# Swapping weights and stream in L0's sums over neighbours, and adding gathered rows on TensorE in L2

## The chip, the cores and the metric

The kernel runs on one core of a Trainium2 chip. The time is the device time of one execution in microseconds (us); the span is what the profile covers from the first instruction to the last. The core's engines each work through their own queue in order: TensorE (PE in the profile; PEld is its loading of weights), VectorE (DVE), ScalarE (ACT), GpSimd (POOL) and SyncE (SP), which here only issues transfers (DMA). A matrix product holds one operand in the array, the weights, and streams the other through it, column by column; its result goes to PSUM. In fp32 each product stands in the profile as two records.

## The reference, cut to what matters

Four layers of a graph network over 3125 nodes with 64 features and 103,125 edges, sorted by destination. Each layer normalizes the running x, applies a relu, runs two passes over the edges, and adds its result to x.

```python
# L0, two passes: a weighted sum over incoming edges, with plain weights W_self, W_neigh
msg = h[src] * edge_weight[:, None]
h_neigh = segment_sum(msg, dst) * inv_deg
h = h @ W_self[l].T + h_neigh @ W_neigh[l].T + b_neigh[l]       # relu after the first
# L1, two passes: m = (h * norm_out)[src] * (a_mu + exp(a_ls) * eps); segment_sum; norm_in, W, b
# L2, two passes, 5 heads of 64 features: attention over incoming edges
xl = (x @ Wl + bl).reshape(n, H, C);  xr = (x @ Wr + br).reshape(n, H, C)
e = leaky_relu(xl[src] + xr[dst], 0.2)
alpha = einsum('ehc,hc->eh', e, att)
a = softmax of alpha over the edges of one destination
out = segment_sum(a[:, :, None] * xl[src], dst).mean(heads) + bias
# L3, two passes: attention with 8 edge types and 4 heads
```

## The kernel before, in words

Edges are cut into tiles of 128 in the order of their destinations. A chunk is a run of tiles whose destinations lie in a window of 128 nodes: 16 tiles in L0 (51 chunks), 18 in L2 (45 chunks), 24 in L1 and L3. The program is written step by step; a scheduler then fixes the order on each engine ahead of the run, apart from instructions that are marked to stay in program order (here DVE's in L0, L1 and L3, by the helper of line 245). On the chip every queue runs in that fixed order.

**L0 gathers nothing.** `dense_pass` runs twice, with l = 0 and 1. For each chunk the first pass builds a dense array `a` of 128 edge slots by 25 blocks of 128 source nodes: `marks` and `factors` make one-hot factors `ol` and `r` on DVE, half a chunk (8 tiles) at a time, in three buffers each; `build` multiplies them (line 603) and ACT copies the result to `a` and the counts to `cnt` (605, 606). `contract` then multiplies `a` by the 25 blocks of the nodes' rows `h_l` (line 612): the 128x128 block of `a` is the weights, 64 features stream. `contracted` copies the sums to `v` (620). `merge` places them in the chunk's window by a product with `sel` (629) and transposes the window's own rows `hw` (633). `carried` passes a sum that crosses a chunk's edge on to the next chunk; `apply` multiplies by the two weight matrices (650, 651) and counts degrees (653); `rows` finishes on DVE and sends `deg` and `hn` to DRAM (545). `red` (line 245) sums `cnt` after each chunk. The first four arrays are kept in SBUF, 47 go to DRAM (`a_d`, 692) and are read again in the second pass (587) into four buffers. Between the passes SP loads `h_l[1]` (736), writes `n_out`, and issues 2 x 34 loads of one column each (`n_out_w`, `n_in`, 740 and 741), after which DVE computes a reciprocal root (743).

**L1** gathers source rows on POOL (line 257), multiplies them by noise `ea` that SP loads, and sums by products (537). Its gather buffers hold 18 groups of four tiles. It needs `n_in` and `n_out_w` only where a chunk's rows are finished.

**L2** treats two tiles at a time (`score`). POOL gathers 400 fp32 values per edge to `g` (nine buffers of six tiles): five heads of 64 scores and two sums each, five more columns, and the node's own features. PE spreads the destination's scores to the edges (`px`, line 983, bf16, 335 columns, PSUM in two buffers). DVE adds `px` to `g` (984), applies relu and the attention vector (986) and sums one head (987); ACT sums the other four heads (991), because `ACT_HEADS = 4`; `top` on DVE (1000) makes `am`. Every nine pairs the chunk is turned (810), scanned on DVE (816, 818, 820 makes `mx`), turned back (822), weighted, and summed on PE by `ao` (254); `heads` and `nodes` finish the nodes' rows, which in the first layer of L2 also get their products for the second (924, 925). **L3** is built in the same way on smaller rows.

Of the kernel before, what the change touches and what calls it, by code (L numbers as in the profile page):

```python
# [8 lines left out]
F32 = mybir.dt.float32  # L9
# [4 lines left out]
OP = mybir.AluOpType  # L14
# [126 lines left out]
def sorted_path(ctx: ExitStack, tc: tile.TileContext, A: dict, out: bass.AP):  # L141
# [54 lines left out]
    a_d = dram.tile([NC0, P, NBK, P], F32, name="a_d")  # L196
# [241 lines left out]
    def spmm_layers():  # L438
        with tc.tile_pool(name="pm", bufs=1) as pm:
# [107 lines left out]
            def dense_pass(lp, l, kept, wT, bias):  # L547
# [8 lines left out]
                with tc.tile_pool(name="dn", bufs=2) as sp, tc.tile_pool(name="dn_ps", bufs=1, space=PSUM) as ps:  # L556
# [25 lines left out]

                    def begin(c):
                        st = dict(c=c, n=tiles0(c), a=kept[c] if c < KEPT_N else sp.tile([P, NBK, P], F32, name="a", bufs=2 if l == 0 else 4))
                        if l:
                            if c >= KEPT_N:
                                nc.sync.dma_start(st["a"], a_d[c])
                        else:
                            if st["n"] < CT0:
                                nc.vector.memset(st["a"], 0.0)  # L590
                            st["oj"], st["wj"] = marks(c)
                            st["f"] = [factors(c, 0, st["wj"])]
                        hw = st["hw"] = sp.tile([P, D], F32, name="hw", bufs=5)
                        nc.sync.dma_start(hw, tabs[l][bass.ds(load_base(c, base0_i), P), :])
                        return st
# [12 lines left out]
                    def contract(st, b):  # L608

                        if b == 0:  # L610
                            st["pv"] = ps.tile([P, D + 1], F32, name="pv", bufs=2)
                        nc.tensor.matmul(st["pv"][:, :D], st["a"][:, b], h_l[l][:, b], start=(b == 0), stop=(b == NBK - 1))  # L612

                    def contracted(st):
                        M = D
                        if l == 0:
                            M = D + 1
                            nc.tensor.matmul(st["pv"][:, D:], st["oj"].rearrange("p t j -> p (t j)"), one, start=True, stop=True)
                        st["v"] = sp.tile([P, D + 1], F32, name="v")
                        nc.scalar.copy(st["v"][:, :M], st["pv"][:, :M])  # L620
                        st["M"] = M
                        sel = st["sel"] = sp.tile([P, P], F32, name="sel")
                        V.tensor_scalar(sel, iota, at0[:, st["c"]:st["c"] + 1], None, op0=OP.is_equal)

                    def merge(st):

                        M = st["M"]
                        acc = ps.tile([P, P], F32, name="acc")
                        nc.tensor.matmul(acc[:M], st["v"][:, :M], st["sel"], start=True, stop=True)
                        st["sums"] = sp.tile([P, P], F32, name="sums", bufs=4)  # L630
                        nc.scalar.copy(st["sums"][:M], acc[:M])
                        pt = ps.tile([D, P], F32, name="pt")
                        nc.tensor.transpose(pt, st["hw"], ident)
                        st["hT"] = sp.tile([D, P], F32, name="hT")
                        nc.scalar.copy(st["hT"], pt)

                    def carried(st):
                        c, M, sums = st["c"], st["M"], st["sums"]
                        if c:
                            picked = sp.tile([P, P], F32, name="picked")  # L640
                            V.scalar_tensor_tensor(picked[:M], iota[:M], step0[:M, c - 1:c], st["before"]["sums"][:M],
# [27 lines left out]
                    KEPT_N = len(kept)  # L669
                    states = {0: begin(0)}  # L670
                    for c in range(NC0 + 4):
                        st, old = states.get(c), states.get(c - 1)
                        if st:
                            st["before"] = old
                        if c + 1 < NC0 and l:
                            states[c + 1] = begin(c + 1)
                        todo = list(range(NBK)) if (old if l == 0 else st) else []
                        of = old if l == 0 else st
                        if l == 0 and st:
                            st["cnt"] = sp.tile([P, CT0, NBK], F32, name="cnt")  # L680
                            pairs = st["n"] // 2
                            for q in range(pairs):
                                if q == 0 and st["n"] > HT:
                                    st["f"].append(factors(c, 1, st["wj"]))
                                if q == min(4, pairs - 1) and c + 1 < NC0:
                                    states[c + 1] = begin(c + 1)
                                build(st, q)
                                for b in todo[:4]:
                                    contract(old, b)
                                todo = todo[4:]  # L690
                            if c >= KEPT_N:
                                nc.sync.dma_start(a_d[c], st["a"])
# [3 lines left out]
                        for b in todo:  # L696
                            contract(of, b)
                        off = 1 if l == 0 else 0
                        late = [states.get(c - off - k) for k in range(4)]
                        if late[3]:  # L700
                            rows(late[3])
                        if late[2]:
                            carried(late[2]), apply(late[2])
                        if late[1]:
                            merge(late[1])
                        if late[0]:
                            contracted(late[0])

            with tc.tile_pool(name="l0", bufs=1) as lp:
                KEPT = 4  # L710
# [1299 lines left out]
```

## Time and profile before

| | |
|---|---|
| median of 10 runs | 8650.73 us (8639.55 to 8659.64) |
| the profiled execution | 8655.86 us, its span 8654.1 us |
| PE, weight loads, DVE, ACT, POOL busy | 54%, 41%, 49%, 28%, 58% of the span |
| L0, first pass | 118 to 866 us from the start of the span |
| L0, second pass | first products at 871.9, last rows at 1588 us |
| L1 | 1588 to 3703 us |
| L2, the pairs of its first and second pass | 3844 to 5110 and 5152 to 6356 us |
| L3, the rest | to 8654 us |
| one gather in L1, mean (line 257) | 974 ns, 0.30 us of issue before each |
| one gather in L3, mean | 984 ns |
| one load of `a` (1.6 MB) in the second pass of L0 | lands about 6.5 us after its issue |

How the profile's lines read: a group names its line, engine and operation, then output and inputs by their names in the program (buffer numbers left out), shapes, and the count; behind the bar stand the busy us, the mean ns of one, the us that the engine stood idle just before them, and what ended that idle time. "Issue" is time in which nothing that the profile shows was waited for. The timeline gives start and length in us. The clock is the share of full speed that TensorE was granted.

### The profile page before, as it was taken

What the parts mean: (1) busy time and instruction counts of PE and PEld (TensorE: products, weight loads), DVE (VectorE), ACT (ScalarE), POOL (GpSimd) and SP (SyncE); (2) the same over time, 40 slices, a digit from 0 to 9 for tenths busy, and PEclk for the clock granted to TensorE, in tenths of its full rate; (3) what the DMA queues carried; (4) which work ended last, traced back from release to release, by engine and by line L of the source; (5) the groups of instructions that cost most, each with busy time, mean ns of one, the idle gap of its engine ahead of it and who ended that gap; (6) DMA issues with size and microseconds to landing.
All of it is one profiled execution on the core that took longest, in us unless ns stands there. A gap on an engine that the chain in (4) does not pass through costs nothing. (4 is left out here: it accounts for less than half of the span.)

```text
span 8654.1 us, 104742 instructions
## 1 busy us (share of the span) xinstructions
PE 4660.8 (54%) x23937; PEld 3564.7 (41%) x23937; DVE 4272.6 (49%) x12144; ACT 2397.4 (28%) x15657; POOL 5044.3 (58%) x4849
## 2 busy tenths in 40 slices
PE   5998799544444444445656555555563444423333
PEld 4997699433333333323333323333342333322222
DVE  5766011222222222269999988888853333333333
ACT  2333000000000000037777767777641111100000
POOL 0000000377777777727777757777727777677776
PEclk8999555555555555555555555555555555555555
DMA  2332333221111111136555545555532222111111
GB/s 64 119 127 104 97 129 135 61 53 53 53 51 51 52 52 52 47 114 172 164 164 161 161 125 162 159 160 159 158 99 44 49 49 49 46 38 40 40 40 39
DMA packets 542968, 799.05 MB, mean 92 GB/s; under 512 B 253426, under 2 KB 386153, under 8 KB 530315
## 3 DMA queue, kind: packets, MB, share of 16 engines
q0 software_dynamic: 206464, 439.52, 20.0%
q1 hardware_dynamic: 335883, 352.72, 12.8%
q8 instruction: 209, 3.42, 0.2%
q14 instruction: 412, 3.38, 0.1%
HBM read 657.39 MB, written 134.39 MB: 91 GB/s over the span
## 5 line engine op out<-in xcount | busy, mean ns | idle before, releaser
L257 POOL DMA_INDIRECT g<-l,idx x1616 | 1574.6, 974 | 2092.0 <-issue 1963.4
L991 ACT ACTIVATE junk<-g 128x66 f32<-128x66 f32 x6448 | 1558.6, 245 | 348.9 <-issue 101.8
L537 PE MATMUL acc<-hit,g 128*128 128x128 f32 x3232 | 838.8, 441 | 1249.8 <-DVE g L245 1249.8
L537 PEld LDWEIGHTS acc<-hit,g 128*128 128x128 f32 x3232 | 719.9, 328 | 1361.8 <-DVE g L245 1309.8
L991 ACT ACTIVATION_READ_ACCUMULATOR junk<-g 128x1 f32 x6448 | 1212.2, 188 | 0.2
L257 POOL DMA_INDIRECT g<-l_0l,src_t x806 | 919.8, 1141 | 464.4 <-issue 197.4
L257 POOL DMA_INDIRECT g<-l_1l,src_t x806 | 961.4, 1193 | 310.1 <-issue 192.9
L257 POOL DMA_INDIRECT g<-l_0v,idx x806 | 793.3, 984 | 388.4 <-issue 216.7
L257 POOL DMA_INDIRECT g<-l_1v,idx x806 | 793.3, 984 | 284.8 <-issue 212.3
L245 DVE TENSOR_TENSOR g<-g,ea 128x256 f32<-128x256 f32 x404 | 179.0, 443 | 1539.0 <-DMA g<-l,idx 1539.0
L984 DVE TENSOR_TENSOR g<-g,px 128x670 f32<-128x670 f32 x806 | 672.3, 843 | 280.2 <-DMA g<-l_1l,src_t 142.3
L612 PEld LDWEIGHTS pv<-h_l,a 128*128 128x128 f32 x4700 | 792.2, 262 | 43.8 <-ACT a L605 28.3
L612 PE MATMUL pv<-h_l,a 128*128 128x64 f32 x4700 | 800.9, 347 | 15.8 <-ACT a L605 13.4
L983 PE MATMUL px<-win,oT 36*128 36x335 bf16 x1612 | 571.8, 459 | 276.6 <-DVE g L984 231.9
L986 DVE SCALAR_TENSOR_TENSOR g<-g,att 128x660 f32<-128x660 f32 x806 | 671.4, 835 | 0.0
L245 DVE TENSOR_TENSOR am<-am,g 128x16 f32<-128x16 f32 x404 | 74.7, 185 | 1001.7 <-DMA g<-l_1v,idx 548.1
L254 PE MATMUL acc<-ao,g 128*70 128x72 f32 x3224 | 442.2, 328 | 207.1 <-DVE ao L1032 103.9
L254 PEld LDWEIGHTS acc<-ao,g 128*70 128x70 f32 x3224 | 399.4, 235 | 334.9 <-DVE ao L1032 206.0
L254 PE MATMUL acc<-oh,g 128*68 128x12 f32 x3224 | 399.0, 268 | 219.7 <-DVE g L245 99.0
L254 PEld LDWEIGHTS acc<-oh,g 128*68 128x68 f32 x3224 | 380.7, 230 | 260.9 <-issue 96.6
L1252 PE MATMUL px<-win,oT 36*128 36x32 bf16 x1612 | 134.4, 191 | 634.0 <-DVE oT L852 589.0
L540 ACT COPY sums<-acc 128x128 f32<-128x128 f32 x68 | 18.1, 266 | 1621.5 <-PE acc L537 1591.2
(327 smaller groups left out, 7319.9 us busy)
## 6 DMA issues: line engine op xcount, KB each, us to landing
a_d<-a SPq DMA_DIRECT2D x47, 1600.0 KB
a<-a_d SPq DMA_DIRECT2D x47, 1600.0 KB
g<-l,idx POOLq DMA_INDIRECT x1616
ea<-in_edge_attr_dram SPq DMA_DIRECT2D x33, 768.0 KB
ea<-in_edge_attr_n_dram SPq DMA_DIRECT2D x33, 768.0 KB
oT<-dl_d SPq DMA_DIRECT2D x88, 162.0 KB
oT<-dl_d SPq DMA_DIRECT2D x66, 216.0 KB
g<-l_0l,src_t POOLq DMA_INDIRECT x806
```

Of the source, the lines that this page charges most:

```text
L245: return tc.keep_in_program_order(op(*args, **kwargs))
L254: nc.tensor.matmul(acc[..., bass.ds(at, width)], lhsT, rhs, start=False, stop=True, skip_group_check=True)
L257: nc.gpsimd.indirect_dma_start(out=to, out_offset=None, in_=table, in_offset=bass.IndirectOffsetOnAxis(ap=idx, axis=0))
L537: nc.tensor.matmul(st["acc"][:M], g[:, k, :], h[:, k, :], start=(i == 0 and k == 0), stop=(end and k == 3))
L540: nc.scalar.copy(st["sums"][:M], st["acc"][:M])
L612: nc.tensor.matmul(st["pv"][:, :D], st["a"][:, b], h_l[l][:, b], start=(b == 0), stop=(b == NBK - 1))
L983: nc.tensor.matmul(px[:, j, :SW], s["oT"][:, q * P:(q + 1) * P], s["win"][:, i, :], start=True, stop=True)
L984: nc.vector.tensor_add(g[:, :, :SW], g[:, :, :SW], px[:, :, :SW])
L986: nc.vector.scalar_tensor_tensor(g[:, :, :F], g[:, :, :F], 0.0, bcast(att08[l], 1, 2), op0=OP.max, op1=OP.mult)
L991: nc.scalar.activation(junk, g[:, j, hd * C2:(hd + 1) * C2], AF.Copy, accum_out=al[:, q0 + j, hd:hd + 1])
L1252: nc.tensor.matmul(px[:, k * H * R:(k + 1) * H * R], s["oT"][:, q * P:(q + 1) * P], s["win"][:, q // 2, :], start=True, stop=True)
```

## The change

In L0, arrays now stand for two chunks, 256 slots wide. `contract` holds the nodes' rows (64 columns) as weights and streams 256 slots, so that the sums come out transposed, 64 by 256, and the new step `turned` turns each half back by a product with the identity. Steps after it follow a table of due times. `a` has two buffers of double size, the loads of `n_in` and `n_out_w` and their roots move from between L0's passes to the start of L1, and `hw` is loaded later. In L2, PE adds the gathered row to `px` by a product with the identity, in fp32, ahead of line 983's; ACT copies the five score columns back to `g`; line 986 reads `px` in PSUM; and `ACT_HEADS` is 3, so that DVE sums two heads and ACT three.

In the order on PE the 25 products of a pair of chunks come in one block after the pair's 32 products of `build` in the first pass of L0; before, 25 of every second chunk came in a block and the others between those of `build`.

```diff
-    a_d = dram.tile([NC0, P, NBK, P], F32, name="a_d")
+    a_d = dram.tile([(NC0 + 1) // 2, P, NBK, 2 * P], F32, name="a_d")
...
                     def begin(c):
-                        st = dict(c=c, n=tiles0(c), a=kept[c] if c < KEPT_N else sp.tile([P, NBK, P], F32, name="a", bufs=2 if l == 0 else 4))
-                        if l:
-                            if c >= KEPT_N:
-                                nc.sync.dma_start(st["a"], a_d[c])
...
+                        p, i = divmod(c, 2)
+                        if i == 0:
+                            arrays[p] = kept[p] if p < len(kept) else sp.tile([P, NBK, 2 * P], F32, name="a", bufs=2)
+                            if l and p >= len(kept):
+                                nc.sync.dma_start(arrays[p], a_d[p])
+                        st = dict(c=c, n=tiles0(c), a=arrays[p][:, :, i * P:(i + 1) * P])
...
-                        hw = st["hw"] = sp.tile([P, D], F32, name="hw", bufs=5)
-                        nc.sync.dma_start(hw, tabs[l][bass.ds(load_base(c, base0_i), P), :])
...
-                    def contract(st, b):
+                    def contract(p, b):
 
                         if b == 0:
-                            st["pv"] = ps.tile([P, D + 1], F32, name="pv", bufs=2)
-                        nc.tensor.matmul(st["pv"][:, :D], st["a"][:, b], h_l[l][:, b], start=(b == 0), stop=(b == NBK - 1))
-
-                    def contracted(st):
-                        M = D
+                            sums_of[p] = ps.tile([D, 2 * P], F32, name="pv", bufs=2)
+                        nc.tensor.matmul(sums_of[p], h_l[l][:, b], arrays[p][:, b], start=(b == 0), stop=(b == NBK - 1))
+
+                    def contracted(p):
+                        v = sp.tile([D, 2 * P], F32, name="vT")
+                        nc.scalar.copy(v, sums_of[p])
+                        sums_of[p] = v
+
+                    def turned(st):
+                        c = st["c"]
+                        M = st["M"] = D if l else D + 1
+                        pt = ps.tile([P, D + 1], F32, name="pn")
+                        nc.tensor.transpose(pt[:, :D], sums_of[c // 2][:, c % 2 * P:(c % 2 + 1) * P], ident[:D, :D])
                         if l == 0:
-                            M = D + 1
-                            nc.tensor.matmul(st["pv"][:, D:], st["oj"].rearrange("p t j -> p (t j)"), one, start=True, stop=True)
-                        st["v"] = sp.tile([P, D + 1], F32, name="v")
-                        nc.scalar.copy(st["v"][:, :M], st["pv"][:, :M])
...
+                            nc.tensor.matmul(pt[:, D:], st["oj"].rearrange("p t j -> p (t j)"), one, start=True, stop=True)
+                        st["v"] = sp.tile([P, D + 1], F32, name="v", bufs=3)
+                        nc.scalar.copy(st["v"][:, :M], pt[:, :M])
+                        sel = st["sel"] = sp.tile([P, P], F32, name="sel", bufs=3)
+                        V.tensor_scalar(sel, iota, at0[:, c:c + 1], None, op0=OP.is_equal)
+                        hw = st["hw"] = sp.tile([P, D], F32, name="hw", bufs=4)
+                        nc.sync.dma_start(hw, tabs[l][bass.ds(load_base(c, base0_i), P), :])
...
-                        acc = ps.tile([P, P], F32, name="acc")
+                        acc = ps.tile([P, 2, P], F32, name="acc")
...
-                        pt = ps.tile([D, P], F32, name="pt")
-                        nc.tensor.transpose(pt, st["hw"], ident)
+                        nc.tensor.transpose(acc[:D, 1], st["hw"], ident)
...
-                    for c in range(NC0 + 4):
+                    lag = 1 - l
+                    np_ = (NC0 + 1) // 2
+                    due = {}
+                    for n in range(2 * (np_ + lag) + 6):
...
+                            todo = [(p, b) for b in (range(NBK // 2) if i == 0 else range(NBK // 2, NBK))]
...
-                                for b in todo[:4]:
-                                    contract(old, b)
-                                todo = todo[4:]
+                                for t in todo[:2]:
+                                    contract(*t)
+                                todo = todo[2:]
...
+                        if 0 <= p < np_ and i == 1:
+                            contracted(p)
+                            both = [states[c] for c in (2 * p, 2 * p + 1) if c < NC0]
+                            for j, s_ in enumerate(both):
+                                for k, f in ((1, turned), (2 + j, merge), (3 + j, carried), (3 + j, apply), (4 + j, rows)):
+                                    due.setdefault((n + k, f), []).append(s_)
...
-                KEPT = 4
-                kept = [lp.tile([P, NBK, P], F32, name=f"kept{c}") for c in range(KEPT)]
+                KEPT = 2
+                kept = [lp.tile([P, NBK, 2 * P], F32, name=f"kept{c}") for c in range(KEPT)]
...
                     if l == 0:
...
                         nc.sync.dma_start(h_l[1], by_block(tabs[1]))
-                        n_out_d, deg_d = tables["n_out"], tables["deg"]
...
-                        for c in range(NCH):
-                            nc.sync.dma_start(n_out_w[:, c:c + 1], n_out_d[bass.ds(load_base(c), P), :])
-                            nc.sync.dma_start(n_in[:, c:c + 1], deg_d[bass.ds(load_base(c), P), :])
-                        with tc.tile_pool(name="nrm", bufs=1) as np_:
-                            nc.vector.tensor_copy(n_in, rsqrt(np_, n_in, [P, NCH]))
...
                     nc.sync.dma_start(by_block(tabs1[0]), h)
+                for c in range(NCH):
+                    nc.sync.dma_start(n_in[:, c:c + 1], deg_d[bass.ds(load_base(c), P), :])
+                    nc.sync.dma_start(n_out_w[:, c:c + 1], n_out_d[bass.ds(load_base(c), P), :])
+                with tc.tile_pool(name="nrm2", bufs=1) as np_:
+                    nc.vector.tensor_copy(n_in, rsqrt(np_, n_in, [P, NCH]))
...
-        ACT_HEADS = 4
+        ACT_HEADS = 3
...
                     for j in range(2):
                         q = q0 + j
-                        nc.tensor.matmul(px[:, j, :SW], s["oT"][:, q * P:(q + 1) * P], s["win"][:, i, :], start=True, stop=True)
-                    nc.vector.tensor_add(g[:, :, :SW], g[:, :, :SW], px[:, :, :SW])
+                        nc.tensor.matmul(px[:, j, :SW], ident, g[:, j, :SW], start=True, stop=False)
+                        nc.tensor.matmul(px[:, j, :SW], s["oT"][:, q * P:(q + 1) * P], s["win"][:, i, :], start=False, stop=True)
+                    nc.scalar.copy(g[:, :, F:SW], px[:, :, F:SW])
                     HV = H - ACT_HEADS
-                    nc.vector.scalar_tensor_tensor(g[:, :, :F], g[:, :, :F], 0.0, bcast(att08[l], 1, 2), op0=OP.max, op1=OP.mult)
+                    nc.vector.scalar_tensor_tensor(g[:, :, :F], px[:, :, :F], 0.0, bcast(att08[l], 1, 2), op0=OP.max, op1=OP.mult)
```

## The prediction

> **What bounds the kernel now.** I read the slices of the span first, to see which engine is full where; then the busy times by stretch, one stretch per pass; then PE's timeline for its pitch, and the costliest groups for L2.
>
> ```profile
> POOL 0000000377777777727777757777727777677776
> PEclk8999555555555555555555555555555555555555
> ```
>
> Tenths of each fortieth of the span. GpSimd (POOL), which issues the gathers, works from L1 on; TensorE's (PE) granted clock is full in the first L0 pass alone.
>
> ```profile
> 126.00:823.00 697.00, 679.59 (x4605) 634.96 (x4603) 481.12 (x911) 261.31 (x939) 0.00 (x0) 1.00 0.29 114
> ...
> 893.50:943.60 50.10, 0.03 (x1) 0.00 (x0) 1.33 (x7) 0.23 (x1) 0.00 (x0) 0.50 0.08 1
> ...
> 946.00:1588.00 642.00, 641.44 (x2801) 596.60 (x2800) 69.23 (x300) 36.58 (x150) 0.00 (x0) 0.50 0.36 126
> ...
> 3844.00:5110.00 1266.00, 757.74 (x3388) 419.96 (x3386) 1150.55 (x3154) 903.98 (x6720) 911.39 (x799) 0.52 0.58 161
> 5152.00:6356.00 1204.00, 700.32 (x3302) 401.75 (x3302) 1041.38 (x2815) 852.74 (x6585) 956.56 (x801) 0.51 0.58 160
> ...
> 4261.84:4265.26 3.42, 3.42 (x26) 2.90 (x25) 3.42 (x9) 2.10 (x17) 2.54 (x3) 0.50 0.59 169
> 4265.26:4268.68 3.42, 2.75 (x24) 1.69 (x22) 3.09 (x9) 1.92 (x11) 3.12 (x2) 1.00 0.46 112
> ```
>
> Columns: stretch, its length, then busy us of PE, weight loads, DVE, ACT, POOL, then clock, DMA share, GB/s. The second L0 pass is busy 641.44 of 642 us and still gets half a clock: busy is not what opens it. Between the passes PE stands 50 us. Between 3844 and 6356 us, L2, VectorE (DVE) leads: 403 pairs of tiles a layer, 1266/403 = 3.14 us and 1204/403 = 2.99 us each, DVE busy 91% and 86%. The last two lines are one of L2's short stays at full clock: one packed stretch at 0.50, then one at 1.00.
>
> ```profile
> 401.24 3.22 PE L603 MATMUL pa<-r,ol 128*128 128x225 f32 x16
> ...
> 418.85 5.79 PE L612 MATMUL pv<-h_l,a 128*128 128x64 f32 x50
> ...
> 1559.90 10.93 PE L612 MATMUL pv<-h_l,a 128*128 128x64 f32 x50
> ```
>
> An fp32 product is two records. At full clock 225 columns take (3.22-0.35)/15 = 0.19 us a record, 0.85 ns a column; 64 columns should take 0.055 us but take 5.79/50 = 0.116, and 0.219 at half clock, because each record first waits for 128 columns of weights. So the second L0 pass streams about half the time only.
>
> ```profile
> L257 POOL DMA_INDIRECT g<-l_1l,src_t x806 | 961.4, 1193 | 310.1 <-issue 192.9 <-DVE rt L802 64.8 <-ACT junk L991 11.6
> L257 POOL DMA_INDIRECT g<-l_0l,src_t x806 | 919.8, 1141 | 464.4 <-issue 197.4 <-DMA l_0r<-rt 136.8 <-DVE ao L1029 42.8
> ...
> L984 DVE TENSOR_TENSOR g<-g,px 128x670 f32<-128x670 f32 x806 | 672.3, 843 | 280.2 <-DMA g<-l_1l,src_t 142.3 <-PE px L983 110.6 <-DMA g<-l_0l,src_t 10.3
> L986 DVE SCALAR_TENSOR_TENSOR g<-g,att 128x660 f32<-128x660 f32 x806 | 671.4, 835 | 0.0
> L983 PE MATMUL px<-win,oT 36*128 36x335 bf16 x1612 | 571.8, 459 | 276.6 <-DVE g L984 231.9 <-DMA win<-l_0r 14.5 <-DMA win<-l_1r 14.1
> ```
>
> In L2 a pair needs two gathers. POOL issues one every 1.27 us in L1 (0.97 + 0.30 of issue), but they grow to 1.14 and 1.19 us here: 2.9 and 3.0 us a pair. POOL stands right behind DVE in the first layer and sets the pace with it in the second.
>
> **The change, part by part.** The sum is made against the profiled execution, 8655.9 us, 5 above the median of the runs.
>
> *L0, second pass.* Weights become 64 columns, the stream 256: 256 x 0.85 = 0.217 us a record at full clock, 0.435 at half, weights hidden behind it. A pair of chunks is 25 x 2 x 0.217 = 10.9 us, or 21.7 at half. The rest of PE's work is 13.06 (pitch of a chunk now) - 10.93 = 2.1 us at half clock, 2.1 a pair at full; two more turns of the 64 x 256 sums and the waits for their copies, by the 64x128 turn and the 0.22 us copy, about 1.1. Pair: 14.1 us, 26 pairs 367. The stream is then near 80% busy, like the packed stretch that opened the clock in L2, so I take full clock. The array's load for two chunks lands 6.5 us after issue for 1.6 MB now, so at most 12 us for 3.2 MB: under 14, hidden. The pass (871.9 to 1588, 716 us) becomes 372 with its ends: **-344**. This holds the 50 us stall: the 68 one-column loads of n_in and n_out_w (0.82 us apiece on SP's queue) move to L1's start, ahead of the first edge-noise load; 18 buffers of four gathers, 90 us of POOL, cover those 56. Without that cover, +56. Bounds: -380 if the turns hide; -60 if the clock stays half (26 x 25.8 + 50 less stall).
>
> [...]
>
> *L0, first pass.* Its clock is full already. Products: 2 x 5.79 becomes 10.9 a pair, -0.7. But the program's order puts all 25 products in a block behind the pair's 32 one-hot products (L603), where today most stand between those. New waits per pair: the last array copy on ACT before the block (0.49 + 0.21, about 0.8); after it copy, turn, copy, turn (1.7 with the turns' own 0.3). In the odd chunk the factors of its second half come late: DVE first reduces the even chunk's counts (0.96 + 0.19), makes rows (0.9) and carries (0.75), two sel (0.5), then ol and r (1.21 + 0.36 + 1.82), in all 6.7 us after the even chunk's copies; PE has 3.2 us of the first half plus 2.5 of small products to do. About 2 us stand. Sum: 27.5 us a pair now, 31.2 after. In that wait PE streams about a third of the time, and L2's lines show a full clock lost on a thin stretch; half speed for one 3.4 us stretch in six pairs of ten adds 1. +4.7 x 26 = **+122**. Bounds: -20 (all covered by DVE running three halves ahead), +225 (a cold stretch each pair and late hw loads, which SP issues behind deg and hn). Eight instead of five row writes are left at the end, 6.3 us each, partly under the last block: **+12**, 0 to +20.
>
> *L2.* Per pair DVE loses L984 (0.77 start to start); L986 reads PSUM instead, as L984 did at the same rate; L987 takes two heads, 132 more elements, +0.14. DVE falls from 2.86 and 2.58 to about 2.25 and 1.95 us. ACT loses two of its eight sums (0.24 each) and gains one copy of 10 columns, by L620's 65 columns at most 0.22: 2.2 becomes 2.0. PE gains two identity products of 335 columns, four records of 0.285 us = 1.14 at full clock, 2.28 at half, two of L983 (at most 571.8/1612 = 0.35 each now, at half) and about 0.45 or 0.9 of sums and heads: 1.95 or at most 3.9 us a pair. At half clock PE would be full, streaming over 85%, which is what the packed stretch shows opening the clock; at 1.95 of 2.8 us it streams some two thirds, like the first L0 pass (64% there by the same count), which kept it. So PE stays below POOL, and POOL bounds: 2 x (0.97 + 0.30) = 2.55 if gathers run as in L1 (DVE 25% busy), 2.9 and 3.0 as now (DVE 90%). DVE would be about 75% busy; between these I take 2.80, which leaves room for waits on mx and ao. **-(0.34 + 0.19) x 403 = -214.** Bounds: 2.55, -415; PE at half clock, 3.9, +673.
>
> [...] The trace only shows that gathers are longer beside a busy DVE.
>
> L1's gathers and L3 are untouched. Sum: 8656 - 344 + 122 + 12 - 214 = 8232; I say **8235 us**.
>
> **The rivals.**
> 1. *L2's clock does not hold* (the other sign). PE at half speed or flickering becomes L2's bound. For it: L2 has 0.52 and 0.51 today, and PE waits in order on DVE's scans, which thins stretches. Against it: the load that opens it. At 3.9 us a pair: 8656 - 210 + 673 = 9119. It decides from 3.33 us a pair on, where L2 gives back L0's 210.
> 2. *Gathers stay long.* POOL keeps 2.9 and 3.0 us: L2 gives about -90; 8355. For it: the second layer already runs at POOL's pace. Against it: less DVE beside them.
> 3. *L0's second pass stays at half clock.* Then -60 in place of -344: 8516. For it: 640 us at 0.50 now; against it: those stream half the time.
>
> **How the numbers follow.** Chances: forecast 0.58, long gathers 0.18, L0 at half clock 0.08, L2's clock 0.13 (of which 0.03 between 3.1 and 3.33 us a pair), others 0.03. The forecast's own range is 8060 to 8420: L0's first pass gives +-100, L2 -140 to +80. The 80% range adds rivals 2 and 3: 8050 to 8530. Faster than before: 0.58 + 0.18 + 0.08 + 0.02 = 0.86; slower 0.11; within 0.2% (17 us, about what a measurement of this kernel can tell) 0.03.
>
> **What would show it.** Clock 1.0 through the second L0 pass, 14 us a pair, and no 50 us gap; 31 us a pair with a hole before each odd chunk's second half in the first; in L2 a clock mostly 1.0, 2.8 us a pair, gathers near 1.05 us and POOL's idle mostly its issue time. Wrong if L2's clock shows 0.5 with PE full, or if L1's first sums come so late that POOL stops.

## The result: 8907 us, 3.0% slower

The changed kernel takes 8907.48 us (median of 8 runs, 8895.67 to 8925.73) against 8651.34 for the kernel before on the same chips (28 runs): a ratio of 1.030, 95% interval 1.0289 to 1.0307. The forecast was 8235 with a range to 8530. The profiled execution has a span of 8917.6 us, 263.5 more than before. By stages, in us of the span:

| stage | before | after | difference | the prediction's term |
|---|---|---|---|---|
| L0, first pass (to the first load of `a` in the second) | 118 to 872 | 117 to 1319 | +447 | +122 and +12 |
| L0, second pass | 872 to 1588 | 1319 to 1695 | -340 | -344 |
| to L1's first product | 1588 to 1628 | 1695 to 1803 | +68 | 0, or +56 without cover |
| L1, first to last product | 2073 | 2072 | -1 | 0 |
| to L2's first pair | 143 | 136 | -7 | 0 |
| L2, both passes with the gap between | 2510 | 2612 | +102 | -214 |
| the rest | 2300 | 2294 | -6 | 0 |

One term of four was right. The slices of the changed kernel, tenths of each fortieth of the span as before:

```profile
PE   4777769534444444449999998999984444433333
...
POOL 0000000077777777726555555666635777767776
PEclk8877779755555555557888887999985555555555
```

PE's clock is no longer full in the first pass of L0 (7 and 8 where it had 8 and 9), it is full in the second, and in L2 it is mostly granted, but there PE is now 9 tenths busy and POOL only 5 or 6. By stretch (PE, weight loads, DVE, ACT and POOL busy, then clock, DMA share, GB/s), the two passes of L0 and the two of L2:

```profile
117.00:1318.60 1201.60, 896.59 (x3524) 671.87 (x3524) 493.80 (x956) 282.41 (x986) 0.00 (x0) 0.79 0.18 69
1318.60:1695.00 376.40, 366.66 (x1708) 220.63 (x1708) 69.11 (x299) 45.14 (x179) 0.00 (x0) 0.99 0.57 219
4011.00:5389.00 1378.00, 1272.95 (x4999) 602.13 (x4999) 934.36 (x2768) 770.92 (x5528) 792.87 (x804) 0.82 0.54 149
5427.00:6623.00 1196.00, 1103.10 (x4911) 535.83 (x4911) 823.38 (x2418) 711.07 (x5387) 780.43 (x803) 0.92 0.58 161
```

The second pass of L0 does what was forecast: clock 0.99, a pair of chunks every 14.4 us (14.1 forecast). The first pass has PE idle a quarter of the time at a clock of 0.79. L2's loss is all in its first pass: 1378 us for 403 pairs of tiles, 3.42 us each (3.14 before); the second takes 1196, 2.97 each (1202 before). PE is busy 92% in both.

**L0's first pass.** A pair of chunks takes 44 to 49 us in the steady part (47.7 in the one shown below), not 31.2. The waits of 200 to 1200 us (waiting engine, tile and line, what ended it; us in all, times, longest):

```profile
DVE oj L245 <- PE pn L629: 502.6, 22, 24.9
...
PE acc L644 <- DMA hw<-l: 107.8, 20, 7.0
...
PE pa L605 <- DVE r L245: 68.0, 22, 3.1
```

DVE, which works in program order, stands 23 us of each pair before it may write `oj`, and what ends that is L629, the product in the new step `turned` that reads an older `oj`. The same in the timeline:

```profile
460.78 0.35 SPq L635 DMA_DIRECT2D hw<-l  x1
...
467.96 0.40 PE L644 MATMUL acc<-ident,hw 128*64 128x128 f32 x1 [5.49 <-DMA hw<-l]
...
476.30 11.01 PE L616 MATMUL pv<-a,h_l 128*64 128x256 f32 x50 [0.58 <-ACT a L607]
...
488.38 0.29 DVE L245 TENSOR_TENSOR oj<-iota,dl 128x128 f32<-128x128 f32 x1 [24.08 <-PE pn L629]
...
492.32 1.87 PE L605 MATMUL pa<-r,ol 128*128 128x225 f32 x4 [3.09 <-DVE r L245]
```

The block of 25 products ends, is turned, and only then does DVE begin the marks of the next two chunks, so PE stands 3.1 us for its first factors. Earlier in the pair it stands 5.5 us for `hw`, whose load SP now issues in `turned`, one step ahead of its use. With each of these two waits the clock falls to half for 10.2 us, at 464.9 and at 492.2 us (between 200 and 1200 us it falls 43 times, 34 of them for 10.2 us): L605's records, 0.190 us apart on the median at full clock, are 0.374 apart there.

**L1's start.** POOL's first gather comes right behind the last step of `n_in`'s root:

```profile
1792.73 0.18 DVE L767 COPY n_in<-rsq_r 128x34 f32<-128x34 f32 x1
1792.98 0.98 SPq L492 DMA_DIRECT2D ea<-in_edge_attr_dram  x2
1793.96 1.10 POOL L257 DMA_INDIRECT g<-l,idx  x1 [1764.22 <-issue]
```

That root waits for the 68 small loads, which leave SP's queue from 1732 to 1790. So the eighteen gather buffers cover nothing: they are not filled before.

**L2.** The costliest groups:

```profile
L998 PE MATMUL px<-g,ident 128*128 128x335 f32 x3224 | 1488.1, 547 | 77.9 <-DVE g L1002 58.3
L257 POOL DMA_INDIRECT g<-l_0l,src_t x806 | 796.3, 988 | 681.3 <-DVE al L1003 294.3
L257 POOL DMA_INDIRECT g<-l_1l,src_t x806 | 784.2, 973 | 457.8 <-issue 189.2
...
L1002 DVE SCALAR_TENSOR_TENSOR g<-px,att 128x660 f32<-128x660 f32 x806 | 676.5, 839 | 366.2 <-ACT g L1000 351.1
```

Gathers did shorten, from 1141 and 1193 to 988 and 973 ns, yet POOL now waits for others. DVE waits 351 us for ACT's copy of the five score columns (L1000). Read alone, this line says that the copy, queued behind ACT's sums, is the new bottleneck. But the copy in turn waits mostly for PE's last product (331 us between 4100 and 5200 us), and PE waits for almost nothing: it is PE's pace that both lines show. Three records of a tile at full clock:

```profile
4601.24 0.83 PE L998 MATMUL px<-g,ident 128*128 128x335 f32 x2
4602.00 0.31 PE L999 MATMUL px<-win,oT 36*128 36x335 bf16 x1
4602.24 0.83 PE L998 MATMUL px<-g,ident 128*128 128x335 f32 x2
```

A tile takes 1.00 us, 2.0 a pair. The next record starts 0.386 and 0.378 us behind the two fp32 ones, where 335 columns at the 0.85 ns of L603 in L0 come to 0.285: each time that fp32 and bf16 products alternate, some 0.1 us is added. It reads as a wait for the weights: the trace has the loading of such weights start within 0.01 us of their own product, but that of a second fp32 record, at 4601.34, 0.28 us before its own. And once a chunk the clock falls. Columns as in the stretches above:

```profile
4608.62:4612.04 3.42, 2.79 (x9) 1.17 (x9) 3.42 (x10) 1.96 (x16) 2.81 (x3) 1.00 0.68 189
4612.04:4615.46 3.42, 2.04 (x8) 0.76 (x6) 3.42 (x15) 2.95 (x25) 2.51 (x4) 1.00 0.63 183
4615.46:4618.88 3.42, 3.10 (x7) 1.57 (x6) 2.80 (x12) 2.59 (x17) 0.65 (x1) 0.50 0.42 120
4618.88:4622.29 3.41, 3.41 (x12) 1.41 (x11) 0.90 (x2) 0.43 (x2) 0.00 (x0) 0.50 0.14 40
4622.29:4625.71 3.42, 3.42 (x14) 1.83 (x12) 2.72 (x9) 1.91 (x13) 1.83 (x2) 0.50 0.15 30
4625.71:4629.12 3.41, 3.41 (x22) 1.73 (x21) 1.87 (x5) 1.72 (x13) 2.50 (x4) 1.00 0.53 151
```

In the second of these PE stands 1.38 us for one small transposition, and the next three stretches run at half clock:

```profile
4615.24 0.29 PE L932 MATMUL ptn<-ident,tr 85*65 85x85 f32 x1 [1.38 <-DVE tr L925]
```

Over the whole first pass (4011 to 5389 us) this wait comes 43 times:

```profile
PE ptn L932 <- DVE tr L925: 56.8, 43, 1.4
```

The clock falls 43 times there too, 42 times right behind a stretch of 3.41 us whose longest wait is this one, and 40 of the falls last 10.2 us.

So the theory for the experiments was: two buffers of `oj` (and, smaller, the late `hw`) in L0's first pass; the memory of a root at L1's start; and in L2 PE as the bound, by gaps between its products and by the clock. The rivals: `hw` alone in L0, the edge noise's loads in L1, and ACT's copy in L2.

### The profile page after: what moved, and what is told of

Same layout as the page of the kernel before. It is cut to its first block, busy times and chain, and to the rows that moved or that the text cites. A ratio compares the mean times of both kernels' runs of the same rounds, so it can differ in the third digit from the quotient of the medians.

```text
span 8917.6 us, 103400 instructions
## 1 busy us (share of the span) xinstructions
PE 5475.2 (61%) x24763; PEld 3498.7 (39%) x24763; DVE 3837.6 (43%) x11338; ACT 2144.6 (24%) x13293; POOL 4741.1 (53%) x4849
## 3 DMA queue, kind: packets, MB, share of 16 engines
q14 instruction: 386, 3.16, 0.1%
## 5 line engine op out<-in xcount | busy, mean ns | idle before, releaser
L998 PE MATMUL px<-g,ident 128*128 128x335 f32 x3224 | 1488.1, 547 | 77.9 <-DVE g L1002 58.3
L1007 ACT ACTIVATE junk<-g 128x66 f32<-128x66 f32 x4836 | 1173.6, 246 | 178.7 <-DVE g L1002 171.2
L257 POOL DMA_INDIRECT g<-l_1l,src_t x806 | 784.2, 973 | 457.8 <-issue 189.2
L1007 ACT ACTIVATION_READ_ACCUMULATOR junk<-g 128x1 f32 x4836 | 907.9, 188 | 0.0
L1002 DVE SCALAR_TENSOR_TENSOR g<-px,att 128x660 f32<-128x660 f32 x806 | 676.5, 839 | 366.2 <-ACT g L1000 351.1
L998 PEld LDWEIGHTS px<-g,ident 128*128 128x128 f32 x3224 | 546.6, 211 | 322.6 <-issue 225.5
L616 PE MATMUL pv<-a,h_l 128*64 128x256 f32 x2400 | 544.9, 382 | 13.3 <-ACT a L607 13.3
L605 PE MATMUL pa<-r,ol 128*128 128x225 f32 x1612 | 476.1, 461 | 83.7 <-DVE r L245 83.3
L999 PEld LDWEIGHTS <-oT 36*128 36x128 bf16 x1612 | 151.2, 94 | 813.1 <-issue 808.8
L605 PEld LDWEIGHTS pa<-r,ol 128*128 128x128 f32 x1612 | 397.7, 256 | 115.4 <-DVE r L245 78.8
```

The source lines that it names most:

```text
L257: nc.gpsimd.indirect_dma_start(out=to, out_offset=None, in_=table, in_offset=bass.IndirectOffsetOnAxis(ap=idx, axis=0))
L605: nc.tensor.matmul(pa[:, j], ol[:, k + j], r[:, k + j], start=True, stop=True)
L616: nc.tensor.matmul(sums_of[p], h_l[l][:, b], arrays[p][:, b], start=(b == 0), stop=(b == NBK - 1))
L998: nc.tensor.matmul(px[:, j, :SW], ident, g[:, j, :SW], start=True, stop=False)
L999: nc.tensor.matmul(px[:, j, :SW], s["oT"][:, q * P:(q + 1) * P], s["win"][:, i, :], start=False, stop=True)
L1002: nc.vector.scalar_tensor_tensor(g[:, :, :F], px[:, :, :F], 0.0, bcast(att08[l], 1, 2), op0=OP.max, op1=OP.mult)
```

## The experiments

The single runs below stand beside runs of the kernel before of 8655.06 us (the first four) and 8651.74 us (the next four).

**One part alone.** L0 and L1 as before, L2 as changed (the L2 lines of the diff):

> L0 and L1 as before, L2 as changed. The trace of the changed kernel has L2's pairs from 4011 to 6625 us, 2614 us, against 2512 before, with TensorE busy over 90% of them. Theory: L2 loses by itself, +102: 8651 + 102 = about 8755 us. Rival: L2's loss comes with the changed L0 (where buffers lie, the state of the clock on entering); then within 20 us of 8651, or below it.

8728.72 us, +74 on the same chip, less than the +102 expected: L2 takes 1377 and 1175 us in its two passes, in the changed kernel 1378 and 1196. Why the second differs by 21 us is open. L2 loses by itself, all of it in the first pass; the rest of the loss is L0's and L1's start.

**L0's first pass.** Six buffers of `oj`, then the load of `hw` moved back to the chunk's begin, then both:

```diff
-                        oj = sp.tile([P, CT0, W0], F32, name="oj")
+                        oj = sp.tile([P, CT0, W0], F32, name="oj", bufs=6)
```

> The changed kernel with six buffers of oj in place of two. Theory: turned reads oj after the block of 25 products, so with two buffers DVE can't mark the next two chunks until the block is done (DVE stands 23 to 24 us a pair), and the block can't be spread between build's products. With six it is spread, a pair of chunks falls from 47.7 us to 31 to 36, the first pass of L0 from 1132 to 830 to 930, the whole from 8907 to about 8600 to 8710. Rival: a pair is long because merge waits 5.5 us for hw and the clock halves after that; then the pair stays above 42 us and the whole above 8760.

```diff
                             st["f"] = [factors(c, 0, st["wj"])]
+                        hw = st["hw"] = sp.tile([P, D], F32, name="hw", bufs=10)
+                        nc.sync.dma_start(hw, tabs[l][bass.ds(load_base(c, base0_i), P), :])
...
-                        hw = st["hw"] = sp.tile([P, D], F32, name="hw", bufs=4)
-                        nc.sync.dma_start(hw, tabs[l][bass.ds(load_base(c, base0_i), P), :])
```

> The changed kernel with hw loaded where a chunk begins, as before the change, in place of where its sums are turned. Theory of the block: hw's wait is a second, smaller cause; the 5.5 us of it go and half of the half-clock stretch behind it, 6 to 9 us of a pair's 47.7, 25 times: 8680 to 8760. Rival (the wait only moves, since DVE's factors end late anyway): under 30 us gained, 8880 or more.

> Both edits. If hw's load is late by itself, both together give 10 to 100 us more than the buffers of oj alone. If the spread block already gives the load time to land, the same as oj alone within 25 us, the first pass of L0 at 28 to 33 us a pair, close to the 27.5 of before.

The buffers alone: 8590.52 us, 317 less than the changed kernel and already faster than before. `hw` alone: 8810.02, 97 less; a pair falls from some 47 to 41.0 us, as expected, but the first pairs (34 to 36 us in both) gain nothing and the second pass is 10 us longer, so that the whole gained less than the range said. Both: 8586.25, the same as the buffers alone. With six buffers, the scheduler spreads the 25 products between those of `build`; a pair takes 32.0 us, and the pass, between 200 and 850 us, reads:

```profile
200.00:850.00 650.00, 650.00 (x2798) 399.48 (x2796) 395.48 (x755) 220.73 (x789) 0.00 (x0) 1.00 0.27 108
```

PE is busy all of the time at full clock, and no wait for `oj`, `hw` or `r` is left. So the two buffers were the cause; the late `hw` was a second one that only the block brought out. The 32.0 us that stand against 28.2 before (in the steady part as well) are PE's own work: in its mixed order L616's records come 0.260 us apart on the mean against 0.226 in the second pass, and L605's 0.236 against 0.219 before.

**L1's start.** On top of the six buffers, the root's two small tiles go to L1's own pool, which stays, and not to one that is closed before the gather buffers are laid out:

```diff
-                with tc.tile_pool(name="nrm2", bufs=1) as np_:
-                    nc.vector.tensor_copy(n_in, rsqrt(np_, n_in, [P, NCH]))
+                nc.vector.tensor_copy(n_in, rsqrt(lp, n_in, [P, NCH]))
```

> As the run with six buffers of oj (8590.5 us), and the root of n_in in memory that stays, not in a pool closed before L1's gather buffers are laid there. Theory: POOL's first gather (at 1793.96 in the changed kernel, 1.2 us after DVE's last step of the root) waits for that memory; it would start some 56 us earlier, right after the write of h, and since POOL's gathers set L1's pace L1 ends about 56 earlier: 8525 to 8545 us. Rival: the edge noise, whose loads stand on SP behind the 68 small ones, is the limit, and the gathers that are ahead give nothing: 8580 to 8600, with L1's first product and its last where they were.

8534.36 us, 56 less. POOL's first gather, at 1461.21 with six buffers of `oj`, now comes at 1403.25:

```profile
1403.25 1.10 POOL L257 DMA_INDIRECT g<-l,idx  x1 [1372.68 <-DMA n_in<-deg]
```

L1's first product moves by 7 us only, since the edge noise is still loaded behind the 68 small loads. But the gathers run ahead meanwhile, and its last product comes 57 us earlier. What stood was the gathers' memory, and POOL sets L1's pace.

**L2.** All on top of six buffers of `oj` (8590.52 us): the steps from `turn` on one pair later; with that, a pair's products in the order identity, identity, bf16, bf16; or, instead of that order, every third pair added on DVE as before the change.

```diff
-                        (11, heads), (13, nodes)] + [(14 + i, f) for i, f in enumerate(end)])
+                        (11, heads), (13, nodes)] + [(15 + i, f) for i, f in enumerate(end)])
```

> As the run with six buffers of oj (8590.5 us), and in L2 the steps from turn on one pair of tiles later, so that PE does not stand 1.4 us for tr (L932). Theory: that wait leaves one thin 3.4 us stretch a chunk, after which the clock is halved for 10.2 us of 30.7; without it the clock stays, the first pass of L2 falls from 30.7 us a chunk to 24 to 27, 45 chunks: -170 to -300, 8290 to 8420. Rival 1: the clock falls anyway (other waits on the scans): less than 60 us gained. Rival 2: ACT's copy of the score columns behind its sums, which DVE waits for, sets the pace and not PE: less than 60 us gained, with the clock at 1.0.

```diff
                     for j in range(2):
                         q = q0 + j
                         nc.tensor.matmul(px[:, j, :SW], ident, g[:, j, :SW], start=True, stop=False)
+                    for j in range(2):
+                        q = q0 + j
                         nc.tensor.matmul(px[:, j, :SW], s["oT"][:, q * P:(q + 1) * P], s["win"][:, i, :], start=False, stop=True)
```

> As l2turn, and in L2 the two products by the identity first, then the two bf16 ones, of each pair. If PE sets the pace of L2 (its two fp32 records of 335 columns start 0.386 and 0.378 us apart at full clock, 0.1 more than their columns take, since weights aren't loaded ahead between fp32 and bf16), two of four such gaps go, 0.2 us a pair: up to -160 over both passes of L2. If PE doesn't set the pace any more, less than 40 from l2turn.

```diff
-                        nc.tensor.matmul(px[:, j, :SW], ident, g[:, j, :SW], start=True, stop=False)
-                        nc.tensor.matmul(px[:, j, :SW], s["oT"][:, q * P:(q + 1) * P], s["win"][:, i, :], start=False, stop=True)
-                    nc.scalar.copy(g[:, :, F:SW], px[:, :, F:SW])
+                        if i % 3 != 1:
+                            nc.tensor.matmul(px[:, j, :SW], ident, g[:, j, :SW], start=True, stop=False)
+                        nc.tensor.matmul(px[:, j, :SW], s["oT"][:, q * P:(q + 1) * P], s["win"][:, i, :], start=i % 3 == 1, stop=True)
+                    if i % 3 == 1:
+                        nc.vector.tensor_add(g[:, :, :SW], g[:, :, :SW], px[:, :, :SW])
+                    else:
+                        nc.scalar.copy(g[:, :, F:SW], px[:, :, F:SW])
-                    HV = H - ACT_HEADS
-                    nc.vector.scalar_tensor_tensor(g[:, :, :F], px[:, :, :F], 0.0, bcast(att08[l], 1, 2), op0=OP.max, op1=OP.mult)
+                    HV = H - ACT_HEADS - (i % 3 == 1)
+                    nc.vector.scalar_tensor_tensor(g[:, :, :F], (g if i % 3 == 1 else px)[:, :, :F], 0.0, bcast(att08[l], 1, 2), op0=OP.max, op1=OP.mult)
```

In these pairs ACT sums four heads and DVE one, as before the change; the expectation's "three" is a slip.

> As l2turn, but every third pair of tiles adds on DVE as before the change (ACT then with three sums, DVE with one). If PE sets the pace at full clock: PE loses 1.5 us in three pairs of 8.3, DVE gains 0.7 in 7: 60 to 150 us faster than l2turn, POOL (1.25 us a gather, 22.5 a chunk) next. If the thinner stream loses the clock, slower than l2turn by 100 or more.

The two passes of L2, the later step first:

```profile
3676.00:4916.00 1240.00, 1157.56 (x4994) 554.93 (x4995) 936.83 (x2756) 756.60 (x5510) 789.44 (x803) 0.91 0.60 166
4950.00:6183.00 1233.00, 1135.38 (x4913) 549.84 (x4914) 829.40 (x2420) 711.06 (x5389) 779.59 (x803) 0.90 0.58 156
```

then with the products in groups:

```profile
3677.00:4796.00 1119.00, 989.22 (x4996) 526.26 (x4995) 926.70 (x2755) 747.20 (x5513) 791.97 (x804) 0.97 0.66 184
4830.00:5946.00 1116.00, 953.79 (x4911) 513.24 (x4912) 820.82 (x2417) 704.24 (x5386) 783.61 (x803) 0.96 0.64 173
```

and with a third of the pairs on DVE:

```profile
3669.00:5044.00 1375.00, 1305.86 (x4458) 618.11 (x4459) 1002.41 (x2897) 800.47 (x5922) 822.69 (x804) 0.61 0.54 150
5082.00:6453.00 1371.00, 1191.57 (x4377) 565.56 (x4377) 908.59 (x2557) 757.88 (x5796) 786.28 (x802) 0.66 0.52 141
```

and of this run one stay at half clock:

```profile
3737.94:3761.83 23.89, 23.01 (x66) 10.80 (x64) 18.46 (x56) 13.51 (x102) 18.40 (x19) 0.50 0.65 172
```

- *Later step*: 8487.95 us, 103 less, a smaller gain than the 170 to 300 expected. The first pass falls from 1382 to 1240 us with its clock from 0.82 to 0.91. But the theory is only half right: the clock does not stay, it still falls 40 times (43 before), now behind waits of `ao`'s products and of L939, and what has changed is that it is halved for 3.4 us each time, 219 us in all, where it was 498. The second pass, 1192 with the buffers alone, is 1233 here.
- *Groups*: 8250.79 us, 237 less again, which is more than the 160 expected; each pass gains about 120. In the trace a pair's six records now start 0.386, 0.282, 0.282, 0.377, 0.153 and 0.233 us apart, 1.71 in all against 2.01: of the gaps between fp32 and bf16 half are left, and the bf16 pair overlaps too. 403 pairs by 0.30 would be 121 us a pass at full clock. That this meets the gain so closely is partly chance: the clock rose as well, PE is busy 168 and 182 us less in the two passes, and at 88% and 85% busy it no longer sets the pace all of the time. But the edit moves PE's products alone, and neither ACT's copy nor DVE's work, so the rival that these set the pace falls.
- *A third on DVE*: 8752.74 us, 265 more than the later step alone, though PE has 536 records less in either pass. Its clock is 0.61 and 0.66, and PE is busy 95% of the first pass. Once a chunk the clock falls and is back only 24 us later (of 30.7), though PE is busy all but 0.9 of these 24 us, and at half clock a record takes about twice the time (0.374 us in place of 0.190 for L605 in the changed kernel). That it is the thinner stream that loses the clock was expected, but is argued: the run also changes the order of work and its waits.

**The sum.** The four edits together; the same without the later step; and the sum with L0's first pass done as before the change (a's 128x128 blocks as weights, chunk by chunk) into arrays of two chunks for the changed second pass:

> The four edits together. Where the kernel before takes its usual 8650 us, and the gains of the single runs add: 8250.8 - 56 = 8195, 8175 to 8215 us. If L2's gain came by chance of one look: 8380 to 8440. On a chip where the kernel before takes 9900 or more: 10400 to 10500 again, which would say nothing on the sum.

> As best1, but L2's steps from turn on where the change had them. If the wait for tr still thins a 3.4 us stretch and halves the clock a third of the time: 60 to 150 us slower than best1, all in the first pass of L2, clock there 0.80 to 0.90. If the order of the products alone gives PE enough room: within 25 us of best1.

> As best1, but the first pass of L0 sums as before the change. It was 108 us faster than best1 twice where L2 stalled, 85 of them in L0's first pass (708 us of build against 793). If that is all L0: 85 to 110 us faster than best1 here too, 8085 to 8115.

The sum: 8196.61 us (8188.62 to 8201.78), ratio 0.946 to the kernel before (0.9448 to 0.9479), within 2 us of the sum of the single gains. With L0's first pass as before: 8099.17 (8092.72 to 8101.78), ratio 0.935 (0.9337 to 0.9368). That pass takes 709 us of build instead of 792, and the second is unchanged (first and second pass):

```profile
200.00:800.00 600.00, 585.53 (x3944) 545.12 (x3942) 420.46 (x806) 226.79 (x814) 0.00 (x0) 1.00 0.31 121
888.00:1256.00 368.00, 361.52 (x1682) 217.30 (x1682) 65.23 (x282) 43.06 (x171) 0.00 (x0) 0.99 0.58 222
```

So of the change in L0, the wider stream pays only in the second pass, where nothing but the sums is done.

Without the later step: 8238.97 us, 42 more than the sum, between the two cases that had been set. The two passes of L2, without and then with the later step:

```profile
3615.00:4820.00 1205.00, 1066.36 (x4998) 562.72 (x4998) 923.68 (x2769) 754.47 (x5528) 788.59 (x803) 0.89 0.62 171
4857.00:5933.00 1076.00, 922.97 (x4914) 501.33 (x4914) 814.90 (x2419) 703.45 (x5388) 800.96 (x802) 0.99 0.66 179
```

```profile
3620.00:4740.00 1120.00, 992.41 (x4994) 527.45 (x4994) 925.92 (x2756) 746.52 (x5511) 789.52 (x804) 0.97 0.67 184
4774.00:5901.00 1127.00, 965.84 (x4912) 522.06 (x4912) 823.66 (x2419) 704.96 (x5388) 783.13 (x803) 0.95 0.63 171
```

With the later step the first pass gains 85 us and the clock 0.08, so the wait for `tr` does lower the clock there; most of L2's repair is the order of the products. The second pass loses 51 us, with the clock at 0.95 in place of 0.99 (it falls 24 times in place of 6). PE's order there is the same but for its last chunk, but DVE's and ACT's are not, since the later step moves the second pass's last steps as well: in 42 of 44 chunks DVE makes `yo` before the first of a chunk's three products for `ao`, where it made it after the second. Whether that lowers the clock was not tried.

**On two other chips** the same three kernels ran as well, and there the kernel before itself takes 10024.92 and 9890.06 us:

> The changed kernel with the four edits that gained: six buffers of oj, n_in's root in memory that stays, L2's steps from turn on one pair later, and L2's products in the order identity, identity, bf16, bf16. If the gains add (L1's 56 us are in another stage than the others): 8250.8 - 56 = 8195, 8175 to 8215 us. If L1's gain is taken back at L2's start: 8240 or more.

> As best1, but the first pass of L0 sums as before the change (a's 128x128 blocks as weights, 64 features as stream, chunk by chunk), into arrays of two chunks that the second pass then reads as changed. If the turns and the wider order of the first pass cost what the runs show (793 us of build against 705 before, TensorE full at clock 1.0 in both): 60 to 100 us faster than best1, 8095 to 8135. If the writes of two chunks at once, or the smaller lag, stall it: no faster than best1.

> The four edits together, on a chip where the kernel before takes its usual 8650 us (on the chip of the run before this it took 10025, with gathers that landed late through all of L2). If the gains of the single runs add: 8250.8 - 56 = 8195, 8175 to 8215 us, 0.945 to 0.950 of before. If L2's gain came by chance of one look: 8380 to 8440.

On the first of them the sum took 10491.55 us (ratio 1.046, 1.0425 to 1.0489) and the version with the old first pass 10382.78 (1.036, 1.0326 to 1.0389); on the second 10465.63 (1.058, 1.0547 to 1.0617) and 10357.02 (1.047, 1.0437 to 1.0498). The version without the later step took 10457.43 and 10504.82 in single runs. So there both are slower than the kernel before. L0's passes are as long as elsewhere, and the old first pass is worth 109 us (97 elsewhere). Most of the lost time is in L2, 1965 and 1932 us for its passes in place of 1120 and 1127, but not all: of the 2243 us by which the sum's profile is longer on the second of these chips, some 1650 are L2's, 270 L1's with its start, and 330 come behind L2. The waits on both chips have a releaser that no profile from the other chips shows; in the first pass of L2 on the second chip:

```profile
ACT sums L1064 <- remote: 351.3, 36, 13.0
...
DVE ao L1046 <- remote: 243.4, 30, 11.0
ACT g L1001 <- remote: 239.3, 35, 11.3
```

"Remote" is something outside of what the profile follows; each of these three steps is held 30 to 36 times in 45 chunks, for 7 to 10 us on the mean, with the durations of the instructions unchanged (L1003 takes 0.84 us here too). Such waits stand in L1 and L3 as well. Late gathers, which an expectation above names, are not it: between 4000 and 5800 us on the first of these chips DVE waits 15 us for gathers to land. What the releaser is, and why the kernel before loses less (some 1370 and 1240 us against its usual time, the sum 2290 and 2270), was not found, and the changed kernel was not run beside them.

## Why the prediction was wrong, point by point

- *L0's second pass, -344*: right, -340, and by its reason. The stream of 256 columns runs at clock 0.99 (0.216 us a record, 0.217 forecast), the weight loads are busy 220.63 of 376.40 us, where they were 596.60 of 642, the 3.2 MB loads are hidden (PE waits for none between 1335 and 1690 us), a pair takes 14.4 us. Rival 3 falls.
- *L0's first pass, +122 with a bound of +225, and +12 for the tail*: wrong, +447 together. The step that failed: "In the odd chunk the factors of its second half come late". The block of 25 products was taken as given, and only the waits within its order were priced; that the block is itself the effect of `oj` having two buffers while `turned` holds them to the end of the block was missed. In its place the trace shows DVE standing 23 us a pair, PE waiting 3.1 us for the first factors and 5.5 for `hw`, and two stretches of half clock. The load of `hw` had been named, but only as part of a bound, and the bound put a single cold stretch into a pair. With six buffers a pair takes 32.0 us, near the 31.2 forecast, but that is luck: PE is full, without the hole that made the forecast's sum, and the 27.5 that the sum starts from, which is about the pass divided by its chunks, is 28.2 in the steady part.
- *The small loads, hidden, or +56 without cover*: the other end held, +68, of which one edit takes back 56. The failed step is "18 buffers of four gathers, 90 us of POOL, cover those 56": buffers cover a stall only if they may be filled, and these were laid over the root's memory.
- *L2, -214*: wrong, +102. The failed step is PE's sum, "1.95 or at most 3.9 us a pair", with the conclusion "So PE stays below POOL, and POOL bounds". Measured, PE is busy 3.16 us a pair in the first pass (1272.95/403) at a clock of 0.82. Two terms were mis-sized: the identity's records, 1.14 forecast against 1.53 at full clock (2 x 0.386 + 2 x 0.378), because their gaps to bf16 were not counted; and "about 0.45" for the rest, where the grouped version at clock 0.96 still has PE busy 2.37 us a pair (953.79/403), 1.71 of them for the pair's own products, so some 0.65. The third is the clock. Rival 1 was the mechanism, down to the waits on DVE that thin a stretch, and near its deciding point of 3.33 us a pair: 3.42 and 2.97. Its chance of 0.13 was too small, since the forecast's argument (two thirds of streaming keep the clock) is about the mean, and here the clock fell behind one thin stretch a chunk (42 of the 43 falls).
- *Gathers*: expected "near 1.05", measured 0.99 and 0.97, as short as in L1 (974 ns), as the lower end of the L2 term had them. L1002 now reads one input from PSUM, and a gather takes 988 and 973 ns where it took 1141 and 1193. What of the change shortened it was not shown, since DVE's busy time fell as well, from 91% and 86% of the two passes to 68% and 69%. Rival 2 falls.
- *DVE and ACT*: forecast 2.25 and 1.95 us a pair for DVE and 2.0 for ACT; measured 2.32 and 2.04 (934.36 and 823.38 by 403), and 1.91 and 1.76. Right, but beside the point.

In L2 three stretches at half clock followed one with PE busy 2.04 of 3.42 us. Weights are loaded while the product before runs between fp32 and fp32 (0.28 us ahead in the changed kernel; 0.282 us a record of 335 columns in the grouped order), and not between fp32 and bf16, where some 0.1 us stands each time.

## What to carry to other kernels

When a step that reads a tile is moved behind other work, count that tile's buffers first: two buffers of a tile of 512 bytes a partition made the scheduler put 25 products in a block, and cost 317 us, more than the change lost in all. Before work is moved to PE, price it with the gaps of its real neighbours, sort products of one type together (0.30 us of a pair's 2.01 here), and look for the thinnest stretch of each period: in these runs the clock fell behind such stretches for 3.4 or 10.2 us, and with a third of the pairs on DVE it stood at half for 24 us once a chunk. A wait that the profile names (here DVE for ACT's copy) is followed to the engine that waits for nothing before it is called the cause.

## What the runs showed of the hardware that was not expected

- Less work for PE was slower: with 536 records fewer in a pass, the clock fell from 0.91 to 0.61 and the pass grew from 1240 to 1375 us; after each fall in the first pass half clock lasted 24 us, with PE busy 23 of them in the one shown.
- Alternating fp32 and bf16 products cost 0.30 us in a pair's 2.01 us; the same four products, sorted, take 1.71.
- L2's second pass, with the same order on PE but for its last chunk and a small shift in DVE's and ACT's, ran in 1076 us at clock 0.99 and in 1127 at 0.95.
- On two of the chips, kernels that gain 5 to 6.5% elsewhere lose 4 to 6%, some three quarters of the time in L2, with waits of 7 to 10 us that the profile can't attribute.
